# Layer 0's reciprocals spread over the partitions by two DMA transfers instead of a product

## The chip, the cores and the metric

The kernel runs on one core of one Trainium2 chip. The metric is the device time of one execution in microseconds (us), the median of several runs. The kernel before takes 924.37 us (three runs, 921.15 to 925.53). A profiled execution of the same kernel takes longer, 1061.9 us from the first to the last instruction; times read from the trace are on that longer scale.

## The reference

Two graph layers act on 2708 nodes with 256 features; `adj` is a weighted, sparse adjacency matrix of 2708 x 2708. Layer 0, which the change touches, computes per node j (cut to what matters):

```python
# per head h (3 of them): one logit per neighbour i, softmax over the row's edges
att = softmax(where(edge_adj > 0, e_plus, NEG_INF), axis=1)
support_h = (att * edge_adj) @ (h @ W_h)
edge_support = sum_h(support_h) / 3
node_support = adj_without_diagonal @ x
x = layernorm(x + diag * (gru(node_support, x) + gru(edge_support, x)))
```

The softmax is written as unnormalised weights, so each destination node needs a sum over its edges of weight times adjacency times features, per head, and the sum of the weights, the denominator. The support is the first divided by the second. Layer 1 is a second attention layer over the same graph with four heads, followed by another layer norm.

## The kernel before

Features lie on the partitions of the result (two halves of 128), destination nodes along the free axis. Destinations are cut into 43 **spans** of W0 = 64 (line 42; the last has 20), and eight spans make a **group** of 512; there are six groups, of which the last has 148 destinations in three spans. For each span the neighbours are collected into **tiles** of 128 rows: a few whole blocks (WHOLE0, line 43) and lists of gathered rows (TILES0, line 44). For each tile:

- `fetch_raw` (line 681) and `fetch_rows` (line 965) bring the adjacency values and the feature rows, by gathers that GpSimd issues, or by plain transfers on SyncE's queue for whole blocks;
- `prepared` (line 984) makes `four` on VectorE and ScalarE: the adjacency values, and the same times each of three head weights, side by side;
- `multiplied` (line 1016) multiplies the rows with `four` on TensorE and adds into the span's **sum bank** in PSUM (`sums[c]`, from a ring of two banks called acc), and adds the weights' counts into a **denominator bank** (`dens[c]`, from a ring of two called db).

When a span's last tile is in, `divided` (line 1045) works on it. VectorE adds up the denominators into `rden` (destinations on partitions, 64 x 3), replaces zeros, multiplies by the number of heads and takes reciprocals. The sums have features on partitions, so every partition needs every reciprocal: VectorE puts them on diagonals (`rden_own`, 64 x 192), TensorE multiplies these by a matrix of ones into a free part of the denominator bank, and ScalarE copies the result, 128 x 192, to `rb`. VectorE multiplies the three heads' sums, read from the sum bank, with `rb` and writes them to the group's `z` in SBUF. ScalarE has meanwhile copied the unweighted sums to `sa`. The sum bank can be reused when both are done.

After a group's last span `cells_and_norm` (line 1084) multiplies `z` with the head matrices (`supports`, line 1092), runs the two recurrent cells, normalises and projects for layer 1. Four groups find part of their gate products already computed and stored in DRAM (XH), and load them into working tiles on SyncE's queue (line 1127); such a load waits until its working tile is free. Group 4 and group 5 compute all of their gates there.

The order on each engine is not that of the source. Every call is noted, and a planner (`issue`, line 228) puts all instructions in order once, before the program is built: it keeps a model of each engine's time (for a transfer 2.2 us and its bytes at 250 GB/s, line 110), and on each engine takes, of what is ready in the model, what has the longest chain of work behind it. The result is a fixed order per engine. On the chip each engine, SyncE's queue too, runs its instructions in that order; an instruction that waits holds all that stand behind it on its engine. In the trace all these instructions carry the line of the recording helper (L217), so groups are told apart by tile names. `f_home` stands for several tiles that share a home in SBUF; z is one of them.

Of the kernel before, what the change touches and what calls it, by code (L numbers as in the profile page):

```python
# [10 lines left out]
F32 = mybir.dt.float32  # L11
# [9 lines left out]
P = 128  # L21
D = 256
KD = D // P
HEADS0 = 3
HEADS1 = 4
# [5 lines left out]
CH = 512  # L31
# [10 lines left out]
W0 = 64  # L42
# [264 lines left out]
def fast_path(ctx: ExitStack, tc: tile.TileContext, i: dict, out: bass.AP, bad: bass.AP):  # L307
# [11 lines left out]
    nc = plan = Plan(tc.nc)  # L319
# [8 lines left out]
    NG = len(groups)  # L328
# [3 lines left out]
    TW = D + 8  # L332
    C65 = C1 + 1
    H65 = HEADS1 * C65
    spans = [
        [(c * w, min(w, N - c * w)) for c in range((N + w - 1) // w)] for w in (W0, W1)
    ]
# [11 lines left out]
    dram = ctx.enter_context(tc.tile_pool(name="f_dram", bufs=1, space=DRAM))  # L349
# [16 lines left out]
    T0 = dram.tile([N, TW], F32, name="f_T0")  # L366
    T1 = dram.tile([N, TW], F32, name="f_T1")

    TS = dram.tile([NG, HEADS1, CH], F32, name="f_TS")

    KEPT = 4
    XH = dram.tile([KEPT * 2 * KD * 3 * P, CH], F32, name="f_XH")
    plan.pitch = {XH.tensor.name: CH, T0.tensor.name: TW, T1.tensor.name: TW, TS.tensor.name: HEADS1 * CH}


    home1 = const.tile([P, 12 * CH], F32, name="f_home1")
# [159 lines left out]
    small, lists = Rings(const, 2), Rings(const, 2)  # L536
# [156 lines left out]
    ap, tiles = Rings(const, 1, home2), Rings(const, 8, home1)  # L693
# [173 lines left out]
    for g, cs in enumerate(groups):  # L867
        w = width[g]
        pe, pf = accs[0], dbs[0]
        c0, nf = base[g] // W0, w // W0  # L870
        for b0 in range(0, NB, 2):
# [25 lines left out]
            for b in pair:  # L897
                if b in cs:
                    p, o = size[b], b * P - base[g]
# [16 lines left out]
            for b in pair:  # L916
                p = size[b]
# [3 lines left out]
            for b in pair:  # L921
                p = size[b]
# [120 lines left out]
    zs = {}  # L1043

    def divided(c):

        d0, w = spans[0][c]
        g = d0 // CH
        at = d0 - base[g]
        acc = sums[c]  # L1050
        rden = small.tile([W0, HEADS0], F32, name="rden")[:w]
        rb = small.tile([P, HEADS0 * W0], F32, name="rb")[:, : HEADS0 * w]
        own = small.tile([W0, HEADS0, W0], F32, name="rden_own")[:w, :, :w]

        if at == 0:
            zs[g] = (
                zp.tile([P, KD, CH], F32, name="sa", bufs=2), zp.tile([P, HEADS0, KD, CH], F32, name="z")
            )
        none = small.tile([W0, HEADS0], F32, name="none0")[:w]
        nc.vector.tensor_reduce(  # L1060
            rden, dens[c][:w, :H3].rearrange("p (s h) -> p h s", s=3), AX.X, ALU.add
        )

        nc.vector.tensor_scalar(none, rden, 0.0, None, op0=ALU.is_equal)
        nc.vector.scalar_tensor_tensor(rden, rden, float(HEADS0), none, op0=ALU.mult, op1=ALU.add)
        nc.vector.reciprocal(rden, rden)
        nc.scalar.copy(
            zs[g][0][:, :, at : at + w],
            acc.rearrange("p (o i) -> p o i", o=KD)[:, :, :w],
        )  # L1070
        nc.vector.tensor_mul(
            own, ident[:w, :w].rearrange("p (o i) -> p o i", o=1).to_broadcast([w, HEADS0, w]),
            rden.rearrange("p (h o) -> p h o", o=1).to_broadcast([w, HEADS0, w]),
        )
        pb = dens[c][:, P : P + HEADS0 * w]
        nc.tensor.matmul(pb, lhsT=ones_f[:w], rhs=own, start=True, stop=True, skip_group_check=True)
        nc.scalar.copy(rb, pb)
        nc.vector.tensor_mul(
            zs[g][1][:, :, :, at : at + w],
            acc.rearrange("p (o i) -> p o i", o=KD)[:, :, w : 4 * w].rearrange("p o (h i) -> p h o i", h=HEADS0),  # L1080
            rb.rearrange("p (h o i) -> p h o i", h=HEADS0, o=1).to_broadcast([P, HEADS0, KD, w]),
        )

# [145 lines left out]
    for n, (c, whole, m) in enumerate(work0):  # L1229
        if n == EARLY:  # L1230
            for k in slot1:
                fetch_mask(k)
        fetch_raw(n)
        fetch_rows(n)
        prepared(n)
        if multiplied(n):
            divided(c)
            d0, w = spans[0][c]
            if d0 + w in (base[g] + width[g] for g in range(NG)):
                cells_and_norm(d0 // CH)  # L1240
# [159 lines left out]
def tile_adj_resnorm(tc: tile.TileContext, i: dict, out: bass.AP):  # L1400
    nc = tc.nc
    with tc.tile_pool(name="guard", bufs=1) as gp:
        bad = gp.tile([P, 1], F32, name="bad")
        fast_path(tc, i, out, bad)
        with tc.tile_pool(name="guard_ps", bufs=1, space=PSUM) as ps:
            one = gp.tile([P, 1], F32, name="guard_ones")
            nc.vector.memset(one, 1.0)
            nc.vector.tensor_scalar(bad, bad, 0.0, None, op0=ALU.is_gt)
            n = ps.tile([1, 1], F32, name="n_bad")
            nc.tensor.matmul(n, lhsT=bad, rhs=one, start=True, stop=True)  # L1410
            flag = gp.tile([1, 1], I32, name="flag")
            nc.vector.tensor_copy(flag, n)
        taken = nc.values_load(flag[0:1, 0:1], min_val=0, max_val=P)
        with tc.If(taken > 0):
            general_path(tc, i, out)
# [436 lines left out]
```

## Time and profile before

| stretch of the trace, us | what runs | length, us | TensorE busy, us | GpSimd busy, us |
|---|---|---|---|---|
| 305 to 791 | layer 0's tiles, the groups' cells between them | 486 | 399.5 | 301.2 |
| 791 to 845 | group 4's cells | 54 | 54.0 | 0 |
| 845 to 856 | the last spans | 11 | 8.0 | 0 |
| 856 to 1062 | group 5's cells, layer 1 | 206 | 154.2 | 86.6 |

Before 305 us the adjacency matrix is read and the lists of neighbours are made. Over the whole span TensorE is busy 80%, VectorE 57%, ScalarE 53%, GpSimd 50%. A busy share is an average over stages: a wait in one stage is worth something only if TensorE, or what feeds it, has nothing else to do then. A line of a group gives busy time, mean length, and the idle time just before its instructions with what ended it. A line of waits gives who waited for whom, the total in us, how often, and the longest.

### The profile page before, as it was taken

To read this page: it belongs to the slowest core of one execution; us is meant where nothing else is said; L and a number is where in the kernel's file an instruction comes from. 1 tells how busy PE (TensorE), PEld (TensorE's weight loads), DVE (VectorE), ACT (ScalarE), POOL (GpSimd) and SP (SyncE) were. 2 spreads that over 40 slices of the span, in tenths; PEclk is the share of its full clock that TensorE was granted. 3 is DMA by queue.
4 is the path that set the end of the run, shared out by engine and by line. 5 is a ranking of instruction groups with operands and counts; after the bars stand their busy time and mean duration, and the time that the engine had idled before them with its cause. 6 is when DMAs were issued, how large, how long until landed. Compare 5 with 4: busy or idle time off the path is not lost.

```text
span 1061.9 us, 13987 instructions
## 1 busy us (share of the span) xinstructions
PE 847.5 (80%) x3911; PEld 518.9 (49%) x3911; DVE 605.2 (57%) x2035; ACT 557.7 (53%) x1568; POOL 530.5 (50%) x613
## 2 busy tenths in 40 slices
PE   5984888396888898859797698788989977977783
PEld 3431333133466653546345454553554557776672
DVE  5772588362155435847284326644841455988893
ACT  4783867374567653637345453553552232244486
POOL 2055557454466676866675565664430013466640
PEclk9996888698979789978897798899899988989996
DMA  8983878454433332433254223332220013545441
GB/s 306 300 266 98 270 247 236 117 151 105 160 102 85 85 90 79 139 95 104 73 168 143 76 60 97 111 97 77 76 78 0 1 41 99 158 127 152 145 120 52
DMA packets 85047, 132.41 MB, mean 125 GB/s; under 512 B 21520, under 2 KB 43880, under 8 KB 84320
## 3 DMA queue, kind: packets, MB, share of 16 engines
q1 hardware_dynamic: 56800, 71.68, 21.8%
q0 software_dynamic: 20320, 45.59, 16.5%
q10 hardware_dynamic: 7840, 14.16, 3.6%
q8 instruction: 33, 0.54, 0.2%
q14 instruction: 54, 0.44, 0.1%
HBM read 113.03 MB, written 21.12 MB: 126 GB/s over the span
## 4 chain that ended last, share of the span: by engine, by line
PE 35%; DVE 11%; issue 6%; ACT 5%; another core or an unknown queue 4%; DMA 2%; POOL 0%; ACTq 0%; DVEq 0%
PE side L217 17%; PE acc L217 12%; DVE f_home L217 7%; PE db L217 5%; ACT four L217 1%; ACT f_home L217 1%; DMA rows<-f_T,f_idx 1%; DVE f_xn L217 1%; DMA raw<-in_adj_dram,f_idx 1%; ACT y L217 1%; DVE four L217 1%; DVE rden L217 0%; PE pl L217 0%; ACT f_xn L217 0%
## 5 line engine op out<-in xcount | busy, mean ns | idle before, releaser
L217 POOL DMA_INDIRECT rows<-f_T,f_idx x254 | 255.6, 1006 | 276.9 <-PE side L217 91.9
L217 PE MATMUL acc<-four,rows 128*128 128x256 f32 (+1 forms) x712 | 214.1, 445 | 32.5 <-ACT four L217 17.6
L217 PEld LDWEIGHTS acc<-four,rows 128*128 128x128 f32 x712 | 147.9, 220 | 75.3 <-ACT four L217 23.7
L217 ACT ACTIVATE four<-four,rows 128x64 f32<-128x64 f32 (+1 forms) x534 | 145.3, 337 | 53.0 <-DVE four L217 17.0
L217 POOL DMA_INDIRECT raw<-in_adj_dram,f_idx x91 | 95.1, 1045 | 50.4 <-DVE f_m L217 26.2
L217 ACT ACTIVATE f_home<-f_home,f_minus_half 128x1024 bf16<-128x1024 f32 (+4 forms) x72 | 70.0, 976 | 50.3 <-remote 26.8
L217 POOL DMA_INDIRECT f_home<-in_adjT_dram,f_idx x67 | 64.5, 962 | 39.0 <-issue 17.1
L217 DVE TENSOR_REDUCE f_found<-f_home 128x16 f32<-128x1024 f32 (+5 forms) x84 | 72.4, 884 | 19.4 <-POOL f_home L217 9.8
L217 PE MATMUL db<-f_home,f_only 128*22 128x512 bf16 (+2 forms) x132 | 42.4, 404 | 46.9 <-ACT f_home L217 40.6
L217 PE MATMUL acc<-f_home,rows 128*65 128x128 f32 (+2 forms) x512 | 68.3, 286 | 11.1 <-DVE f_home L217 6.8
L217 POOL DMA_INDIRECT f_xn<-in_adjT_dram,f_idx x63 | 63.8, 1012 | 22.4 <-issue 17.4
L217 ACT ACTIVATE f_home<-f_home 128x1024 bf16<-128x1024 f32 (+4 forms) x72 | 62.9, 881 | 21.3 <-PE acc L217 8.1
L217 PE MATMUL side<-f_home,f_edge_wi 128*128 128x512 f32 (+1 forms) x144 | 62.7, 579 | 9.4 <-DVE f_home L217 5.3
L217 PEld LDWEIGHTS acc<-f_home,rows 128*65 128x65 f32 (+1 forms) x512 | 57.3, 144 | 18.1 <-DVE f_home L217 8.9
L217 PE MATMUL side<-f_home,f_node_wi 128*128 128x512 f32 (+1 forms) x144 | 62.3, 566 | 4.1 <-DVE f_home L217 4.1
L217 PE MATMUL side<-f_home,f_gat_w 128*128 128x512 f32 (+1 forms) x144 | 59.1, 569 | 3.8 <-DVE f_home L217 3.8
L217 DVE TENSOR_TENSOR f_home<-f_home,side 128x512 f32<-128x512 f32 (+1 forms) x56 | 36.6, 657 | 44.7 <-PE side L217 29.7
L217 DVE SCALAR_TENSOR_TENSOR f_home<-pl,rows,f_m 128x128 f32<-128x128 f32 x196 | 55.5, 341 | 9.9 <-DMA rows<-f_T,f_idx 5.4
L217 PE MATMUL db<-f_home,rows 128*65 128x128 f32 x376 | 51.5, 289 | 8.7 <-DVE f_home L217 7.3
L217 ACT ACTIVATE m<-four 128x64 bf16<-128x64 f32 (+1 forms) x181 | 40.9, 247 | 26.4 <-DVE four L217 21.2
L217 DVE SCALAR_TENSOR_TENSOR f_home<-ls,rows,f_m 128x128 f32<-128x128 f32 (+1 forms) x168 | 46.6, 339 | 4.8 <-PE side L217 2.8
L217 PEld LDWEIGHTS db<-f_home,rows 128*65 128x65 f32 x376 | 41.9, 143 | 14.9 <-DVE f_home L217 9.4
(221 smaller groups left out, 1458.9 us busy)
## 6 DMA issues: line engine op xcount, KB each, us to landing
f_home<-in_adjT_dram SPq DMA_DIRECT2D x50, 512.0 KB
f_XH<-kept ACTq DMA_DIRECT2D x48, 256.0 KB
f_home<-f_XH SPq DMA_DIRECT2D x48, 256.0 KB
f_home<-f_TS SPq DMA_DIRECT2D x5, 1024.0 KB
rows<-f_T SPq DMA_DIRECT2D x33, 132.0 KB
rows<-f_T,f_idx POOLq DMA_INDIRECT x254
f_T<-f_home SPq DMA_DIRECT2D x21, 132.0 KB
f_T<-in_x_dram SPq DMA_DIRECT2D x3, 896.0 KB
```

The costliest lines, as they stand in the source:

```text
L217: call = lambda: f(*args, **kwargs)
```

## The change

For all groups but the last, the reciprocals go to all partitions by way of DRAM: SyncE's queue writes `rden` (64 x 3) to a small DRAM tensor `f_TD`, and a second transfer, which waits for the first, reads these 192 numbers back onto each of the 128 partitions as `rb`. The diagonals, the product with ones and the copy of its result fall away. ScalarE copies the three heads' sums from the sum bank to `z` without waiting for the reciprocals, so that the bank depends on ScalarE alone, and VectorE multiplies `z` by `rb` in place. `rb` has a ring of three tiles, not two; the order of its 192 numbers is destination, then head. The last group's three spans are done as before.

```diff
+    TD = dram.tile([len(spans[0]) * W0, HEADS0], F32, name="f_TD")
...
-        rb = small.tile([P, HEADS0 * W0], F32, name="rb")[:, : HEADS0 * w]
-        own = small.tile([W0, HEADS0, W0], F32, name="rden_own")[:w, :, :w]
+        rb = small.tile([P, HEADS0 * W0], F32, name="rb", bufs=3)[:, : HEADS0 * w]
...
+        z = zs[g][1][:, :, :, at : at + w]
+        if g < NG - 1:
+
+            nc.sync.dma_start(TD[d0 : d0 + w, :], rden)
+            nc.scalar.copy(z, of_heads)
+            nc.sync.dma_start(
+                rb, bass.AP(tensor=TD.tensor, offset=TD.offset + d0 * HEADS0, ap=[[0, P], [1, w * HEADS0]])
+            )
+            nc.vector.tensor_mul(
+                z, z, rb.rearrange("p (o i h) -> p h o i", h=HEADS0, o=1).to_broadcast([P, HEADS0, KD, w])
+            )
+            return
+        own = small.tile([W0, HEADS0, W0], F32, name="rden_own", bufs=1)[:w, :, :w]
...
         nc.vector.tensor_mul(
-            zs[g][1][:, :, :, at : at + w],
-            acc.rearrange("p (o i) -> p o i", o=KD)[:, :, w : 4 * w].rearrange("p o (h i) -> p h o i", h=HEADS0),
+            z, of_heads,
             rb.rearrange("p (h o i) -> p h o i", h=HEADS0, o=1).to_broadcast([P, HEADS0, KD, w]),
         )
```

`of_heads` names the part of the sum bank that holds the three heads.

More of the change, by code (lines that the diff above doesn't have):

```diff
@@ L372, in fast_path @@
     XH = dram.tile([KEPT * 2 * KD * 3 * P, CH], F32, name="f_XH")
-    plan.pitch = {XH.tensor.name: CH, T0.tensor.name: TW, T1.tensor.name: TW, TS.tensor.name: HEADS1 * CH}
+    TD = dram.tile([len(spans[0]) * W0, HEADS0], F32, name="f_TD")
+    plan.pitch = {TD.tensor.name: HEADS0, XH.tensor.name: CH, T0.tensor.name: TW, T1.tensor.name: TW, TS.tensor.name: HEADS1 * CH}
     home1 = const.tile([P, 12 * CH], F32, name="f_home1")
@@ L1070, in divided @@
         )
+        of_heads = acc.rearrange("p (o i) -> p o i", o=KD)[:, :, w : 4 * w].rearrange(
+            "p o (h i) -> p h o i", h=HEADS0
+        )
[8 more added lines that the diff above has]
+                z, z, rb.rearrange("p (o i h) -> p h o i", h=HEADS0, o=1).to_broadcast([P, HEADS0, KD, w])
+            )
+            return
+        own = small.tile([W0, HEADS0, W0], F32, name="rden_own", bufs=1)[:w, :, :w]
         nc.vector.tensor_mul(
```

## The prediction

> **What bounds the kernel now.** I read the page's busy shares first, then busy time by stretches, then the engines' groups and waits of the stretch that the change touches, and last one span's chain in the timeline. The span sums of layer 0, and so the whole change, lie between 305 and 856 us of the profiled 1061.9 us; the timed runs last 924.37 us, so I scale what I find in the trace by 924.37 / 1061.9 = 0.870.
>
> Busy time by stretches (columns: start and end, length, then busy us and count for TensorE, its weight loads, VectorE, ScalarE, GpSimd; granted clock; DMA share; GB/s):
>
> ```profile
> 305.00:791.00 486.00, 399.53 (x1611) 249.94 (x1609) 263.72 (x889) 255.33 (x901) 301.21 (x296) 0.88 0.34 97
> 791.00:845.00 54.00, 54.00 (x128) 24.51 (x127) 13.41 (x22) 11.11 (x19) 0.00 (x0) 0.98 0.01 3
> 845.00:856.00 11.00, 7.96 (x41) 5.59 (x40) 9.99 (x37) 5.32 (x17) 0.00 (x0) 0.94 0.02 6
> ```
>
> TensorE is busy 82% of the first stretch and 100% of the second, where group 4's cells run alone. VectorE (54%) and ScalarE (53%) have room. GpSimd looks like 62%, but each of its gathers is followed by 0.30 us of issue, so 292 gathers of about 1.25 us make 365 us, 75%: the next limit, not far off. Groups of TensorE and ScalarE in 305 to 856 us (busy, mean ns, then the idle time before and what ended it):
>
> ```profile
> L217 PE MATMUL db<-rden_own,f_ones_f 64*128 64x192 f32 x84 | 26.1, 403 | 10.1 <-DVE rden L217 3.5 <-DVE rden_own L217 3.3 <-issue 3.2
> L217 ACT COPY rb<-db 128x192 f32<-128x192 f32 x42 | 12.9, 313 | 38.4 <-PE db L217 15.2 <-remote 10.8 <-issue 6.6
> L217 DVE TENSOR_TENSOR f_home<-acc,rb 128x384 f32<-128x384 f32 x42 | 22.8, 551 | 25.7 <-ACT rb L217 22.2 <-ACT f_home L217 1.1 <-issue 1.1
> L217 DVE TENSOR_TENSOR rden_own<-f_ident,rden 64x192 f32<-64x192 f32 x42 | 14.4, 348 | 0.4
> ```
>
> The first line is the product that spreads the reciprocals: 26.1 us of TensorE for 42 spans, 0.62 us each, and 10.1 us of idle time in front of it. Of the waits of TensorE in this stretch, two belong to the same chain:
>
> ```profile
> PE acc L217 <- DVE f_home L217: 10.1, 6, 6.9
> PE db L217 <- ACT rb L217: 1.0, 1, 1.0
> ```
>
> The tile view of rb puts the sum bank's share at 10.7 us for TensorE ("PE acc", 7 times). One span's chain shows why (start, length, engine, operation, and in brackets the idle time before):
>
> ```profile
> 503.34 0.29 PE L217 MATMUL db<-rows,m 128*64 128x9 bf16 x4
> 503.68 0.16 DVE L217 TENSOR_REDUCE rden<-db 64x3 f32<-64x9 f32 x1 [0.34 <-PE db L217]
> 504.71 0.35 DVE L217 TENSOR_TENSOR rden_own<-f_ident,rden 64x192 f32<-64x192 f32 x1
> 508.37 0.59 PE L217 MATMUL db<-rden_own,f_ones_f 64*128 64x192 f32 x2
> 514.29 0.32 ACT L217 COPY rb<-db 128x192 f32<-128x192 f32 x1 [3.10 <-PE acc L217]
> 514.64 0.56 DVE L217 TENSOR_TENSOR f_home<-acc,rb 128x384 f32<-128x384 f32 x1
> ```
>
> From the last count (503.63) to the end of the division (515.20) the span's sum bank, one of two, stays taken for 11.6 us.
>
> **What the Trainium skill says.** "DMA: Bandwidth & Descriptors", section on the anatomy of one DMA: some 2.0 us fixed per transfer, mostly the write's receipt, so a read that must wait for a write pays twice. Here the trace bears it out: after layer 0 the last rows of T1 have been issued by 868.18 and the gather that reads them begins at 870.50, 2.3 us; that gather lands in 2.73 us by the chain of work. "VectorE: DVE Perf Modes", section on the errata: ScalarE from PSUM to SBUF takes 172 cycles and one per element at 1.2 GHz. For 192 elements that is 303 ns; the trace has 313. So for 384, which no row here shows, 463 ns is my estimate. The same section gives (N + 151) / 0.96 ns for an fp32 tensor_tensor; 691 ns at 512, the trace 684 to 687, so 557 at 384 where both operands now lie in SBUF, against 551 from PSUM: no change.
>
> **The change part by part.** Five of the six groups, 40 of 43 spans, change.
> - TensorE loses 40 products, 40 x 0.62 = 25 us of busy time. TensorE is the limit for 82% of the stretch, so I count 25 x 0.82 = 20 us.
> - The waits attached to them end: 10.1 us in front of the product, 1.0 us of "PE db <- ACT rb", for the denominator bank whose free part ScalarE still had to copy. What TensorE runs next may be late itself, so I count half of the 11.1, 5 us, rounded down.
> - The sum bank is free after two ScalarE copies (0.26 and 0.46 us), not at the end of the chain: of the 10.7 us that TensorE waited for it I count 6, as half of what waits there also waits for new weighted masks (TensorE's longest wait in the stretch is 17.6 us for these). Copies and rb's ring of 3 are the only price.
> - VectorE loses 40 x 0.348 = 14 us (rden_own); ScalarE changes a 0.313 us copy for one of 0.463, 40 x 0.15 = 6 us more. Both engines are near 54%, and neither sets the end; zero.
> - SyncE issues 80 more transfers, each of some 0.3 us, and has room: by its own view of waits it stands 213.6 us waiting for VectorE to release buffers; zero for the engine. Bytes: 40 x (0.8 KB + 98 KB) = 4 MB against 97 GB/s in the stretch and over 250 GB/s early in the kernel; zero.
> - The new wait: the multiplication on VectorE needs the write's receipt and the read, 2.3 + 2.7 us and two issues of 0.3 us: 5.6 us after the reciprocal (bounds: 1.6 us twice the 0.8 us minimum round trip that the same page gives in its section on latency, and 9 us if each transfer takes double because of the 256 KB loads of kept gates queued ahead). Who waits behind it: the next weighted masks ("four") on VectorE, and so ScalarE, TensorE. In the changed program's order on VectorE there are 7 to 44 instructions between a reciprocal and its multiplication, 14 in the middle; 889 in 486 us are one per 0.55 us, so 14 are 7.7 us and cover it. Eight of the 40 have 10 or fewer, 5.5 us or less, and are short by 0 to 2 us; some others sit on SyncE behind gate loads that wait for buffers. I put 12 us of new VectorE waits, half of it reaching TensorE: 6 us lost.
> - Group ends: the products of the heads need the last span's z. In the changed order 2 to 5 tiles of the next group stand before them (1 to 2 before the change), each four products of 0.45 us, 1.8 us, so 3 more tiles are 5.4 us of useful work over the transfers; zero. The last group keeps its product, since nothing is left to hide a transfer there.
>
> Sum in the trace: 20 + 5 + 6 - 6 = 25 us. GpSimd takes some of it: its rows wait on the same buffers, and 486 - 25 = 461 us leaves it 79% occupied, so I take off a fifth: 20 us. Times 0.870: 17.4 us. Forecast 924.4 - 17.4 = 907 us.
>
> **Rivals.**
> - All of it comes through: 25 us of products, 10.1 and 10.7 us of waits, no new ones: 46 x 0.87 = 40, 884 us. For: TensorE 82% busy. Against: masks and gathers also end TensorE's waits.
> - The gathers become the limit: GpSimd's 75% occupancy leaves room, but its own waits ("rows" for row buffers, 34.8 us) do not all shrink; half of the forecast, 924.4 - 9 = 915 us.
> - The DMA wait takes the product's place: 40 multiplications each short by 1.5 us are 60 us on VectorE, of which 25 reach TensorE, and cancel the 25 gained: about 924 us. For: VectorE's wait for rb (22.2 us) exists already and only changes its source. Against: the distances above.
> - Slower: SyncE is in order and waits for buffers (the 213.6 us above); if reads of rb stand behind such loads at most spans, VectorE stalls by 3 us in 25 of 40 spans, 75 us, of which 40 reach TensorE: 25 + 5 + 6 - 40 = -4, and the reshuffled order of gathers adds as much again: some 8 x 0.87 = 7 us, 931 us.
>
> **How the numbers follow.** Forecast (895 to 914) 0.50; everything comes through 0.10; gathers 0.12; wash 0.12; slower 0.16. Faster by over 0.5% (below 919.8): 0.50 + 0.10 + 0.12 = 0.72; same 0.12; slower 0.16. The range takes in forecast, gathers and wash and reaches toward both ends: 888 to 930.
>
> **What would show it.** Right: products db<-rden_own only 6 records; "PE acc <- DVE f_home" near zero and replaced by short waits on ScalarE copies; TensorE's stretch before group 4's cells some 20 us shorter with 25 us less busy; VectorE waiting for rb in few, short pieces (12 us); the 54 us of group 4's cells unchanged. Wrong: VectorE idle before the multiplication by 40 us or more, SyncE holding rb's reads behind loads of kept gates, GpSimd's gathers back to back, or a first stage (to 300 us) that changes although nothing in it was edited, because the planner ranks all work anew.

## The result and the profile after

The kernel after takes 948.63 us (945.77 to 951.28) where the kernel before takes 924.7 us (921.15 to 925.53): a ratio of 1.0266 with a 95% interval of 1.0221 to 1.0311. It is slower by 2.7%; the prediction had 907 us and a range of 888 to 930, and gave "slower" 0.16.

In some sets of runs every kernel, the one before too, takes 1053 to 1111 us, with idle pieces of up to 20 us for which the trace shows no work to wait for, so each ratio below is to the kernel before in the same set and leaves out runs over 1.5% above the fastest of their kernel. The profile that the prediction read (1061.9 us) is such a long one; the profile of before used from here on spans 927.6 us. A long idle piece, in another profile of the kernel before, of 1092.6 us (start, length, instruction, and in brackets the idle time in front):

```profile
79.67 0.62 ACT L217 ACTIVATE f_home<-f_home 128x512 bf16<-128x512 f32 x1
97.46 1.15 ACT L217 ACTIVATE f_home<-f_home,f_minus_half 128x1024 bf16<-128x1024 f32 x1 [17.17 <-remote]
```

Where the time goes can be bounded by two events of the trace: the first span's denominators are added up, and group 4's cells begin (the first product with `f_gat_w`). Ahead of the first and behind the second little changes: the first lies at 258.8 us before and 257.3 after, and from the second to the same event of group 5 it is 74.6 and 74.9 us. Between the two lie 417.5 us before and 435.7 after (columns as in the prediction: busy us and count for TensorE, weight loads, VectorE, ScalarE, GpSimd; clock; DMA share; GB/s). The kernel before:

```profile
258.80:676.30 417.50, 374.32 (x1599) 235.05 (x1600) 263.82 (x887) 253.06 (x896) 299.14 (x293) 0.95 0.40 112
```

The kernel after:

```profile
257.30:693.00 435.70, 363.68 (x1551) 232.41 (x1549) 255.74 (x849) 259.13 (x909) 301.63 (x300) 0.92 0.57 117
```

TensorE is busy 10.6 us less and idle 28.8 us more (72.0 against 43.2). The DMA engines' share rises from 0.40 to 0.57 although they move hardly more bytes per second, 117 against 112 GB/s. The groups that the change touches, before:

```profile
L217 PE MATMUL db<-rden_own,f_ones_f 64*128 64x192 f32 x84 | 25.7, 397 | 7.3 <-DVE rden_own L217 7.2
L217 DVE TENSOR_TENSOR f_home<-acc,rb 128x384 f32<-128x384 f32 x42 | 22.8, 551 | 20.3 <-ACT rb L217 18.6 <-ACT f_home L217 1.4
```

and after:

```profile
L217 DVE TENSOR_TENSOR f_home<-f_home,rb 128x384 f32<-128x384 f32 x40 | 27.0, 678 | 54.8 <-DMA rb<-f_TD 38.4 <-ACT f_home L217 14.4 <-ACT four L217 1.9
L217 ACT COPY f_home<-acc 128x384 f32<-128x384 f32 x40 | 18.6, 466 | 4.8 <-PE acc L217 4.5
```

The 80 records of the product are gone, the ScalarE copy has come, and VectorE's idle time in front of the division has gone from 20.3 to 54.8 us, 38.4 of it for the read of `rb`. Waits by who waited for whom (us in total, times, longest), before:

```profile
ACT four L217 <- DMA rows<-f_T,f_idx: 26.0, 24, 5.5
PE acc L217 <- ACT four L217: 9.7, 13, 1.4
```

and after:

```profile
SPq L217 <- DMA f_TD<-rden: 83.9, 34, 4.8
ACT four L217 <- DMA rows<-f_T,f_idx: 40.8, 30, 3.7
DVE f_home L217 <- DMA rb<-f_TD: 38.4, 22, 4.5
PE acc L217 <- ACT four L217: 23.6, 22, 3.1
```

Besides VectorE's wait for `rb`, SyncE stands 84 us for the receipts of the writes, and a wait has grown in which none of the new transfers takes part: ScalarE for gathered rows, and TensorE for what ScalarE makes of them. The queues of the two kernels show why (packets, MB, share of the 16 DMA engines' span); before:

```profile
q1 hardware_dynamic: 56800, 71.68, 25.0%
q0 software_dynamic: 20320, 45.59, 19.3%
```

after:

```profile
q1 hardware_dynamic: 65760, 75.65, 28.8%
q0 software_dynamic: 20320, 45.59, 23.1%
```

q0 carries GpSimd's gathers. It has the same packets and bytes in both, but they take 23.1% of 945.0 us instead of 19.3% of 927.6: times 16 engines and over 20320 packets, 172 ns for one instead of 141. The new transfers are the 8960 packets more in q1, 224 for each of 40 spans. Two runs told of below make only one of the two transfers; they have 60000 and 62560 packets in q1, so 80 of the 224 belong to the write and 144 to the read.

One span's chain of work after, to be read against the one in the prediction (start, length, what), shows the new path from reciprocal to division:

```profile
498.91 0.18 DVE rden L217
499.09 0.02 issue
499.10 3.98 DMA f_TD<-rden
503.08 0.02 issue
503.10 5.21 DMA rb<-f_TD
```

The timeline has the division at the end of it, and the next span's reciprocal and transfers:

```profile
504.14 0.17 DVE L217 RECIPROCAL rden<-rden 64x3 f32<-64x3 f32 x1
504.34 0.45 SPq L217 DMA_DIRECT2D f_TD<-rden  x1
508.40 0.68 DVE L217 TENSOR_TENSOR f_home<-f_home,rb 128x384 f32<-128x384 f32 x1 [3.78 <-DMA rb<-f_TD]
508.53 0.32 SPq L217 DMA_DIRECT2D rb<-f_TD  x1
```

From the reciprocal's end, 499.09, to the division, 508.40, 9.3 us pass, and VectorE stood still for the last 3.78. SyncE meanwhile could pass nothing from 504.79, when the second write was issued, to 508.53, when its receipt let the second read go. Nine such trips on the chain between 480 and 700 us have a mean of 4.6 us for the write and 4.0 for the read.

### The profile page after: what moved, and what is told of

It is laid out like the page before. It is cut to its first block, busy times and chain, and to the rows that moved or that the text cites. A ratio compares the mean times of both kernels' runs of the same rounds, so it can differ in the third digit from the quotient of the medians.

```text
span 945.0 us, 13977 instructions
## 1 busy us (share of the span) xinstructions
PE 793.3 (84%) x3831; PEld 491.7 (52%) x3831; DVE 597.4 (63%) x1995; ACT 558.4 (59%) x1567; POOL 531.4 (56%) x613
## 3 DMA queue, kind: packets, MB, share of 16 engines
q1 hardware_dynamic: 65760, 75.65, 28.8%
q0 software_dynamic: 20320, 45.59, 23.1%
## 4 chain that ended last, share of the span: by engine, by line
PE 42%; DMA 21%; DVE 16%; ACT 8%; issue 7%; POOL 5%; SPq 0%; ACTq 0%; DVEq 0%; POOLq 0%
PE side L217 19%; PE acc L217 13%; DVE f_home L217 10%; PE db L217 9%; DMA f_TD<-rden 6%; DMA rb<-f_TD 5%; DMA rows<-f_T,f_idx 5%; POOL f_m L217 3%; DMA raw<-in_adj_dram,f_idx 3%; ACT four L217 2%; ACT f_home L217 2%; PE pl L217 1%; ACT y L217 1%; DMA f_home<-in_L_gnn_gat_a_dram 1%; DVE f_xn L217 1%
## 5 line engine op out<-in xcount | busy, mean ns | idle before, releaser
L217 PE MATMUL acc<-four,rows 128*128 128x256 f32 (+1 forms) x712 | 202.5, 427 | 28.0 <-ACT four L217 23.6
L217 PEld LDWEIGHTS acc<-four,rows 128*128 128x128 f32 x712 | 142.2, 211 | 77.9 <-ACT four L217 32.5
L217 POOL DMA_INDIRECT f_home<-in_adjT_dram,f_idx x67 | 65.7, 980 | 20.3 <-issue 15.7
L217 DVE TENSOR_TENSOR f_home<-f_home,rb 128x384 f32<-128x384 f32 x40 | 27.0, 678 | 54.8 <-DMA rb<-f_TD 38.4
L217 PE MATMUL side<-f_home,f_node_wi 128*128 128x512 f32 (+1 forms) x144 | 59.8, 547 | 1.3 <-DVE f_home L217 1.3
L217 PE MATMUL side<-f_home,f_edge_wi 128*128 128x512 f32 (+1 forms) x144 | 57.9, 545 | 0.0
L217 PE MATMUL db<-f_home,rows 128*65 128x128 f32 x376 | 49.3, 283 | 5.8 <-DVE f_home L217 5.8
L217 DVE TENSOR_TENSOR f_home<-f_home,side 128x512 f32<-128x512 f32 (+1 forms) x56 | 36.6, 657 | 17.9 <-PE side L217 17.5
L217 PE MATMUL acc<-f_home,f_home 128*9 128x512 bf16 (+2 forms) x132 | 40.0, 385 | 8.9 <-ACT f_home L217 8.9
```

What stands on the lines that cost most here:

```text
L217: call = lambda: f(*args, **kwargs)
```

## The experiments

In kernels said to have "the order kept", the planner is told of the same operations as in the kernel it is made from, so every engine has the same order; only what is issued in their place differs. They leave something out or read fixed numbers, which is said of each. Medians of all runs, and ratios to the kernel before of the same set:

| run | before, us | this, us | ratio (95%) |
|---|---|---|---|
| after, again | 922.31 | 951.69 | 1.0287 (1.0232 to 1.0343) |
| early copy only | 922.31 | 922.18 | 0.9983 (0.9958 to 1.0007) |
| before, without the product | 922.31 | 915.16 | 0.9925 (0.988 to 0.997) |
| transfers made, none waits | 925.74 | 941.16 | 1.0178 (1.0114 to 1.0243) |
| transfers left out | 925.74 | 914.85 | 0.9898 (0.9873 to 0.9923) |
| read need not wait for the write | 925.74 | 941.91 | 1.0204 (1.0137 to 1.027) |
| transfers priced in the planner | 925.74 | 937.74 | 1.0113 (1.0074 to 1.0152) |

A ratio is not quite the quotient of the two medians beside it: for the read that need not wait, four runs between 932 and 948 us, that quotient is 1.0175. The runs of the longer sets have no line here; their ratios stand with them below. My theory at this point was that the waits for the round trip, VectorE's above all, cost the time; the rivals were the changed order and the transfers' presence as such.

**Removing each wait, order kept.** Three kernels. The first reads `rb` from other data, so that the read doesn't wait for the write; the second makes both transfers but divides by fixed numbers, so that VectorE waits for neither; the third leaves the transfers out as well. (All three divide by other numbers than the reference's.)

```diff
+            other = bass.AP(tensor=x.tensor, offset=x.offset + c * D, ap=[[0, P], [1, w * HEADS0]])
-            nc.sync.dma_start(
-                rb, bass.AP(tensor=TD.tensor, offset=TD.offset + d0 * HEADS0, ap=[[0, P], [1, w * HEADS0]])
+            plan.note(
+                "sync", "dma_start", lambda to, _: tc.nc.sync.dma_start(to, other),
+                (rb, bass.AP(tensor=TD.tensor, offset=TD.offset + d0 * HEADS0, ap=[[0, P], [1, w * HEADS0]])), {},
             )
```

```diff
-            nc.vector.tensor_mul(
-                z, z, rb.rearrange("p (o i h) -> p h o i", h=HEADS0, o=1).to_broadcast([P, HEADS0, KD, w])
-            )
+            of_rb = lambda v: v.rearrange("p (o i h) -> p h o i", h=HEADS0, o=1).to_broadcast([P, HEADS0, KD, w])
+            fixed = of_rb(gat_w[:, 0, 0, : HEADS0 * w])
+            plan.note(
+                "vector", "tensor_mul", lambda to, v, _: tc.nc.vector.tensor_mul(to, v, fixed), (z, z, of_rb(rb)), {}
+            )
```

```diff
-            nc.sync.dma_start(TD[d0 : d0 + w, :], rden)
+            plan.note("sync", "dma_start", lambda to, v: None, (TD[d0 : d0 + w, :], rden), {})
...
-            nc.sync.dma_start(
+            plan.note(
+                "sync", "dma_start", lambda to, v: None,
...
```

They ran first, beside a profile of the kernel before, in a set in which the kernel before takes 1086 us.

> The kernel before, unchanged, profiled a second time. Its first profile spans 1061.9 us where its timed runs last 924; that of the changed kernel spans 945.0 where its runs last 949. If the first profile was stretched, this one should span some 920 to 930 us, with about 465 us or less from the first sums to group 4's cells, and gathers spaced more tightly. If it spans 1060 again, profiling costs this kernel 140 us that it doesn't cost the changed one.

> The changed kernel with the order of every engine kept, in which the transfer to rb reads 192 numbers of the input x and so doesn't wait for the write of the reciprocals (the result is then divided by other numbers). Both transfers are still made. Latency theory (waits for the round trip hold VectorE and the ends of the groups): SyncE's 84 us of waits for the write go, rb comes some 4 us earlier, so about half of the loss returns and more: 920 to 935 us. Traffic theory (the 80 small transfers slow down the gathers): no change, 945 to 950. Order theory (the planner's new order is the loss): 940 to 950.

> The changed kernel with the order of every engine kept and both transfers made, but VectorE multiplies by fixed numbers (a row of the head weights) and so waits for no transfer (the result is then not divided by the sums of weights). Latency theory: the whole loss and the hoped for gain appear, 900 to 915 us. Traffic theory: 940 to 950, since the transfers are all there. Order theory: 940 to 950.

> As the run before, and the two transfers of each span are left out too; the order of every engine is kept. What it gains over the run before is the traffic and SyncE's waits. Latency theory: within 5 us of the run before, 900 to 912. Traffic theory: 900 to 915, some 30 us below the run before. Order theory: 935 to 950, since nothing but the order is left of the change.

They gave 1.0187 (1.0082 to 1.0293), 1.0092 (1.0062 to 1.0122) and 0.9914 (0.9867 to 0.996). The same three kernels, in a set in which the kernel before takes 925.74 us, with a fourth that is told of further below:

> The changed kernel, order of every engine kept, both transfers made, VectorE multiplying by fixed numbers so that it waits for neither (the result is not divided by the sums of weights); the same kernel as the second of the first set, now beside runs of some 925 us. Latency theory (38 us of VectorE's waits for rb, and TensorE's behind them): ratio 0.98 to 0.995, the whole 2.7% gone. Traffic theory (the DMA share rose from 0.39 to 0.57 in the stretch, ScalarE's waits for gathered rows from 26.0 to 40.8 us): 1.02 to 1.03. Order theory: 1.02 to 1.03.

> As the run before, with both transfers of each span left out as well, order kept. Latency theory: 0.98 to 0.99, within 0.005 of the run before. Traffic theory: 0.98 to 0.995, at least 0.02 below the run before. Order theory: 1.01 to 1.03, as there is nothing left but the order and the copies. What this run and the one before differ by is the price of the traffic.

> The changed kernel, order kept, both transfers made, rb read from the input x and so not after the write (the result is divided by other numbers). The wait for the write's receipt, some 4.6 us of the 8.6 us round trip, goes. Latency theory: half of the loss or more returns, ratio 1.00 to 1.015. Traffic and order theory: 1.02 to 1.03.

The third, with the transfers left out, is 1.0% faster than before in the order of the kernel after: the order isn't what costs. Making the transfers, with no engine but SyncE waiting for them, takes it from 0.9898 to 1.0178, 941.16 - 914.85 = 26.3 us. The wait of VectorE, which the theory had made the main cost, is what remains from 1.0178 to the 1.0266 and 1.0287 of the whole change: 0.9 to 1.1%, 8 to 10 us. That is a rough figure, since it compares sets whose ratios are each uncertain by some 0.5 points. So the theory falls; the presence of the transfers costs most. In the kernel without transfers the stretch up to group 4's cells reads

```profile
258.80:660.60 401.80, 349.04 (x1557) 221.95 (x1555) 257.54 (x855) 258.92 (x912) 307.39 (x299) 0.97 0.43 117
```

33.9 us less than after: TensorE is idle 52.8 us, not 72.0, and its 1557 products are 14.6 us shorter than the 1551 after, at a granted clock of 0.97 against 0.92. The waits tell the same; where transfers are made and none waits for them:

```profile
SPq L217 <- DMA f_TD<-rden: 87.9, 34, 5.0
ACT four L217 <- DMA rows<-f_T,f_idx: 50.3, 32, 9.0
```

where they are left out:

```profile
ACT four L217 <- DMA rows<-f_T,f_idx: 22.5, 26, 2.8
```

where the read doesn't wait for the write:

```profile
ACT four L217 <- DMA rows<-f_T,f_idx: 49.0, 29, 3.7
DVE f_home L217 <- DMA rb<-in_x_dram: 10.3, 12, 2.3
```

The last kernel has no wait of SyncE for receipts at all, 28 us less of VectorE's wait, and is still 1.0204; the wait for gathered rows stays at twice its length. Its SyncE still stands for the reciprocals that it writes, 67.1 us in 19 waits, against 35.0 us in 14 in the kernel after.

**The change's parts without the transfers.** Beside the kernels before and after, one that only takes the early copy over (ScalarE copies the heads' sums to `z`, VectorE multiplies there, the product stays; the planner gives it an order of its own), and one that takes the product, its diagonals and its copy out of the kernel before, order kept, for the five groups, and divides by fixed numbers.

```diff
         nc.scalar.copy(rb, pb)
+        if g < NG - 1:
+            nc.scalar.copy(z, of_heads)
         nc.vector.tensor_mul(
-            zs[g][1][:, :, :, at : at + w],
...
+            z, z if g < NG - 1 else of_heads,
```

```diff
...
-        nc.tensor.matmul(pb, lhsT=ones_f[:w], rhs=own, start=True, stop=True, skip_group_check=True)
-        nc.scalar.copy(rb, pb)
+        plan.note(
+            "tensor", "matmul", lambda *of, **how: tc.nc.tensor.matmul(*of, **how) if kept else None,
+            (pb,), dict(lhsT=ones_f[:w], rhs=own, start=True, stop=True, skip_group_check=True),
+        )
+        plan.note("scalar", "copy", lambda *of: tc.nc.scalar.copy(*of) if kept else None, (rb, pb), {})
...
```

> The kernel before, profiled once more. On another chip its time was 1086 us, 17% above the 924.7 us of the comparison with the changed kernel, and its profile showed engines idle for up to 20 us with nothing in the trace to wait for. If this run's time is near 925, its profile is the one to lay beside that of the changed kernel (945.0 us): layer 0's sums should then take about 440 to 450 us, and the gathers should stand at most 1.3 us apart where they are the limit.

> The changed kernel again, beside the others of this set. A ratio of 1.02 to 1.03 if the chip behaves as in the first comparison; where runs last 1080 us and more, long idle pieces hide waits that end at the same time, and the ratio should lie nearer 1, 1.00 to 1.02.

> One part of the change alone: ScalarE copies the heads' sums out of their bank at once and VectorE divides them in place, while the reciprocals are spread by the product as before. Latency theory: the part without transfers can only help, by the bank's waits (10.7 us counted before), less some 6 us of ScalarE: ratio 0.985 to 1.00. Order theory: anything from 0.98 to 1.03, since the planner ranks all work anew. Traffic theory: as the latency theory.

> The kernel before with the order of every engine kept, and for five of six groups without the diagonals, the product and the copy of its result; VectorE multiplies by fixed numbers instead (the result is not divided by the sums of weights). This is the most that taking the product out can give, with nothing in its place. The prediction counted 31 us in the trace before new waits, some 27 us timed: ratio 0.965 to 0.975. If the product hides beside GpSimd's gathers, 0.985 to 1.00, and the gain that the prediction set against the new waits was never there.

The copy alone changes nothing that can be measured (0.9983). Taking the product out with nothing in its place gains 0.75%, 7 us (the interval allows 3 to 11), of 25.7 us of TensorE's busy time and 7.3 us of waits in front of it. In this order, that is the most the change had to gain from this part; the kernel without transfers (0.9898) has the early copy and the new order too, and gains 11 us by the medians; the intervals overlap.

**The transfers' times told to the planner.** The planner counts 2.2 us and the bytes for a transfer. Given 2.4 us more for the write and 1.8 for the read, it puts more instructions between a reciprocal and its division: 24 in the middle of VectorE's order, not 14. The longer times also count in its ranking of chains. This kernel computes all.

```diff
+    def more(op):
...
+        return 2.4 if op.out.startswith("f_TD") else 1.8 if op.out.startswith("rb") else 0.0
...
-                end = moved
+                end = moved + self.more(op)
```

> The changed kernel complete, with the planner told that the write takes 2.4 us and the read 1.8 us longer than any transfer does in its model (4.6 and 4.0 us from issue to landing, as the trace of the changed kernel has them). In the new order 24 instructions stand between a reciprocal and its multiplication on VectorE in the middle of the spans, 14 before. Latency theory: most of the loss was that the order allows the transfers too little time, so 0.99 to 1.01. Traffic theory: 1.015 to 1.03.

It is the best of the complete kernels with the transfers, 1.0113, and still slower than before. The tile view of `rb` in its profile has what is left of VectorE's wait in front of the division (us, times):

```profile
  DMA rb<-f_TD: 0.2, 1
```

and the waits have ScalarE's for the rows:

```profile
ACT four L217 <- DMA rows<-f_T,f_idx: 45.8, 22, 4.0
```

So the order can hide the round trip from VectorE entirely. The gathers' wait remains, and so do 69.3 us of SyncE's waits for receipts. The gain over the kernel after, 1.5 points, is larger than the 0.9 to 1.1 put down to VectorE's wait above; every engine has a new order here, and no run separates that from the shorter wait.

**Which transfer, and what of it.** Over all runs, a gather's packet (share of q0 times span times 16, over 20320) takes:

| what the queue carries for 40 spans | ns per gather packet |
|---|---|
| none of the transfers | 141, 138 and 141 (before; the last two in longer sets), 143 (early copy), 142 (no product), 145 and 143 (transfers left out) |
| write of 64 rows of 12 bytes and read | 172 and 169 (after), 179 and 171 (none waits), 171 and 161 (read at once), 180 (planner) |
| the same write of constants, and a read that waits for nothing | 166 |
| write of 64 rows of 12 bytes alone | 182, 166 |
| read alone, one row onto 128 partitions | 147 |
| read alone, 128 different rows of 768 bytes | 145 |
| write of one row of 768 bytes, and read | 138 |

The five last lines are kernels made for this, order kept, dividing by fixed numbers; as the kernel that leaves both out, with one or both transfers issued again, from or to other places. Writes alone and reads alone take over one of the diffs above each; for the reads of 128 rows the source's step from partition to partition is `D`, not 0. In the first of the five, traffic alone, the write takes constants, and nothing on SyncE waits for a reciprocal or a receipt:

```diff
-            nc.sync.dma_start(TD[d0 : d0 + w, :], rden)
+            plan.note(
+                "sync", "dma_start", lambda to, _: tc.nc.sync.dma_start(to, ident[:w, :HEADS0]),
+                (TD[d0 : d0 + w, :], rden), {},
+            )
```

In the last, the write is one long row of constants, the read waits for it, and VectorE waits for neither:

```diff
-            nc.sync.dma_start(TD[d0 : d0 + w, :], rden)
+            line = bass.AP(tensor=TD.tensor, offset=TD.offset + d0 * HEADS0, ap=[[w * HEADS0, 1], [1, w * HEADS0]])
+            plan.note(
+                "sync", "dma_start", lambda to, _: tc.nc.sync.dma_start(line, gat_w[0:1, 0, 0, : w * HEADS0]),
+                (TD[d0 : d0 + w, :], rden), {},
+            )
```

> The changed kernel, order kept, both transfers of each span made with the same bytes and shapes, but the write sends constants and the read takes numbers of the input x, and VectorE multiplies by fixed numbers: neither SyncE nor VectorE waits for them (the result is not divided by the sums of weights). Traffic theory: as with nobody waiting for data, 1.012 to 1.02. Queue theory (SyncE's waits for reciprocals and for the write hold the loads behind them): 0.99 to 1.00, as without transfers.

> Order kept, the write of the reciprocals made, the read left out, VectorE multiplying by fixed numbers (the result is not divided by the sums of weights). The write is 64 rows of 12 bytes. Traffic theory, if the small rows are what loads the DMA engines: 1.01 to 1.02. If the read does: 0.99 to 0.995. Queue theory: 0.995 to 1.005, as SyncE still waits for the reciprocals but not for the write.

> Order kept, the write left out, the read made from one row of the input x onto all partitions with nobody waiting, VectorE multiplying by fixed numbers (the result is not divided by the sums of weights). 128 packets of 768 bytes. Traffic theory, if the read loads the DMA engines: 1.01 to 1.018. If the write does: 0.99 to 0.995. Queue theory: 0.99, nothing is waited for.

> As the run before, but each partition reads another row of x, 768 bytes of it; bytes and packets are the same (the result is not divided by the sums of weights). If it is the one row read 128 times at once that holds the DMA engines: back to 0.99 to 0.995. If it is packets and bytes: as the run before.

> The changed kernel, order kept, both transfers made and the read waiting for the write, but the write sends 768 bytes of constants from one partition as one row in place of 64 rows of 12 bytes, and VectorE multiplies by fixed numbers (the result is not divided by the sums of weights). If the small rows hold up the gathers: gather packets at 143 to 150 ns, the ratio at 0.99 to 1.00 although SyncE still waits for every write. If any write does, or the reads: 165 ns and more, 1.01 to 1.02 where runs last 925 us. If SyncE's waits for the write were the cost: 145 ns, but 1.01 or more.

> The write alone again, order kept, 64 rows of 12 bytes, no read, VectorE multiplying by fixed numbers (the result is not divided by the sums of weights). Small rows theory: gather packets at 175 to 185 ns as before, and where runs last 925 us a ratio of 1.005 to 1.02. If the read or SyncE's waits for the write were needed for the loss: 0.99 to 1.00 at the same packet time.

The packets settle which transfer lengthens them: the write in 64 rows of 12 bytes lengthens the gathers' packets from a mean of 142 ns to between 161 and 182, by 13 to 28%, whoever waits for it; the reads (145 and 147), and the same 768 bytes written as one row (138), hardly do. "DMA: Bandwidth & Descriptors" in the Trainium skill states under Specifications that below 512 bytes the engine reads, modifies and writes. No run here shows that step itself, and the write as one row makes 2 packets where the small rows make 80, so the size of the rows and their number are not told apart. What the table adds is that another queue's packets pay.

The times don't settle how much of the 26 us that is. These ran where the kernel before takes 1094 and 1072 us: traffic alone 0.9977 (0.9945 to 1.0009), writes alone 1.0028 (0.9995 to 1.0061) and, the same kernel in the second set, 1.0097 (1.0062 to 1.0133), reads alone 0.9951 (0.9905 to 0.9997), reads of rows 0.9958 (0.9927 to 0.9988), long row 1.0146 (1.01 to 1.0192). By the medians of all runs the long row would be 1.0051, and in the first set the transfers left out 1.0052 and not 0.9914: these ratios cannot rank the kernels. As they stand, traffic alone has the slow packets and no loss; the long row has fast packets, SyncE still waiting for receipts (14.7 us), and a loss. Read so, the cost would be SyncE's queue standing still; but at 925 us the kernel whose SyncE waits for no receipt lost 1.0204 - 0.9898 = 3.1%, about 1.1 points of which the 10.3 us of VectorE's wait could explain at most. That does not exclude the held queue, because SyncE stands for the reciprocals there. One and the same kernel differs by 0.007 between two such sets, as much as what is to be told apart.

The traces of the 925 us set say where the loss arrives. Up to group 4's cells, all engines together wait 24.6 us for gathered rows where the transfers are left out, and 51.9 where they are made and none waits for them; for everything that SyncE's own queue carries they wait 2.4 and 10.2 us. On the chain of work of that stretch, a gather takes a mean of 3.4 us from issue to landing in the first (14 gathers) and 4.9 in the second (16). So most of the loss reaches the engines through the gathers, and little through loads held up on SyncE. That it is the longer packets that make the gathers late fits this, but is not shown: in the longer sets traffic alone has the long packets, and ScalarE waits 17.4 us for rows there, against 17.9 with the transfers left out. None of the five kernels ran at 925 us, so the split between slower gathers and SyncE's held queue stays open.

## Why the prediction was wrong

The prediction set a gain of 31 us in the trace against a loss of 6. Of the gain 7 to 11 us exist; of the loss, the transfers' presence alone makes 26 us, and VectorE's wait for them 8 to 10. The steps that failed are the two zeros for the transfers, as bytes and as work on SyncE's queue, and the size of the product's term. How the 26 us divide between the two zeros stays open.

- **"20 us" for the product: mis-sized, by about a factor of three.** TensorE's busy time did fall as said, but "the limit for 82% of the stretch" took a busy share for a share of the path. With nothing in the product's place the timed gain is 7 us, where 20 and the 5 for its waits came to 25 x 0.87 = 22. Between before and the kernel without transfers TensorE's busy time falls by 25.3 us up to group 4's cells and its idle time rises by 9.6: part of the gain becomes waiting.
- **"6" for the sum bank: nothing.** The mechanism is there ("PE acc <- DVE f_home", 4.3 us up to group 4's cells, is gone in the kernel with the early copy alone, with 0.3 us for ScalarE's copy in its place), but that kernel is 0.9983. TensorE waits for the weighted masks instead, 19.4 us and not 9.1, as the step half allowed.
- **"Bytes: 4 MB against 97 GB/s ... zero": the first step that failed.** The write is 0.8 KB, but 64 rows of 12 bytes in 80 packets, and the transfers' presence costs 26 us with no engine but SyncE waiting for them. Bandwidth was not the resource: 117 GB/s after, 112 before, while the DMA engines' share rose from 0.40 to 0.57, the gathers' packets grew from 142 ns to between 161 and 182, and the waits for gathered rows doubled.
- **"SyncE has room ... zero for the engine": failed as an argument, of open size.** 213.6 us of standing for buffers isn't room in a queue that runs in order: it now stands 84 us for receipts as well. What engines wait for on that queue's other transfers is small, 10.2 us against 2.4.
- **"5.6 us after the reciprocal": too short.** 4.6 + 4.0 us, near the upper bound of 9. The 2.3 us came from the stretch after layer 0, where no gathers ran. Fourteen instructions, 7.7 us, then don't cover it; VectorE waited 38.4 us, not 12, and by the difference above 8 to 10 us, not 6, reach the time.
- **"Group ends: zero": failed.** Before group 4's cells (start, length, instruction) the kernel before needs 2.9 us from the last reciprocal to the first product:

```profile
673.45 0.16 DVE L217 RECIPROCAL rden<-rden 64x3 f32<-64x3 f32 x1
674.75 1.02 DVE L217 TENSOR_TENSOR f_home<-acc,rb 128x384 f32<-128x384 f32 x2 [0.55 <-ACT rb L217]
676.33 1.45 PE L217 MATMUL side<-f_home,f_gat_w 128*128 128x512 f32 x3
```

  The chain of work after has both transfers there (the last reciprocal began at 683.14):

```profile
683.57 4.69 DMA f_TD<-rden
...
688.27 3.95 DMA rb<-f_TD
...
692.25 0.67 DVE f_home L217
...
692.99 7.20 PE side L217 x11
```

  That is 9.9 us, and in the 11 us from 682.5 TensorE is idle for 3.6, where the kernel before is idle 0.4 us in the 13 from 664.5.
- **"557 ... no change" for VectorE's division: 678 ns.** In place with `rb` in its old order (the early copy alone) it is 553, so the prediction's price held for the move from PSUM to SBUF. The 125 ns come with the new order of `rb`, read at every third number: with fixed numbers at the same step and no transfers, it is still 675. 40 x 0.125 = 5 us on an engine with room. ScalarE's copy, 463 ns by the prediction's estimate from the Trainium skill, "VectorE: DVE Perf Modes" (errata), is 466.
- **Times 0.870: a wrong scale.** It spread the 138 us between the profile and the timed runs evenly over the trace. The stretch of 486 us is 417.5 in a profile that spans as long as the timed runs; there TensorE is busy 90%, not 82, and the 365 us that the prediction counted for GpSimd's gathers would be 87%, not 75: the next limit stood nearer than it looked.
- The slower rival named SyncE's order and got 931 us from waits alone; it had the right sign, but it too had no term for the transfers' traffic. Group 4's cells (54.0 us of TensorE in both) and the first stage stayed as predicted, and the product is left with its six records.

In sum, as ratios to before: everything but the transfers -1.0%, their presence +2.8, the division's wait for them +0.9 to 1.1; together +2.7 to 2.9. The last of the three is the remainder, not measured alone.

## What to carry to other kernels

Price a transfer by its rows and packets and by what else runs on the DMA engines and stands in its queue, not by its bytes alone, and take the length of a trip from a stretch with the same traffic. Before replacing an operation, ask what the kernel gains with nothing in its place: an engine's busy share is an upper bound, and here the prize was 7 us, or 11 with the early copy and the new order. See that a profile's span agrees with the timed runs before scaling from it.

## What the runs showed that I had not expected

- Forty small writes to DRAM in 64 rows of 12 bytes make the 20320 packets of another queue 13 to 28% longer (161 to 182 ns against a mean of 142); as one row each they do not (138 ns).
- An fp32 operand read at a stride of 12 bytes costs VectorE 678 ns for 128 x 384 results where the same multiplication in order takes 553.
- TensorE's granted clock was 0.913 to 0.921 in all eight runs of the kernel after and 0.928 to 0.948 in those of the kernel before near 925 us; its products of 128 x 256 (TensorE's largest group) took a mean of 431 ns after, 423 before and 401 with the transfers left out, in 258 to 658 us. The Trainium skill, "TensorE: Matmul & The Clock Gate", Part 1, says that the clock follows how busy the engine has been. The kernel after fits that up to group 4's cells (72.0 us idle at 0.92, before 43.2 at 0.95), but the kernel with the transfers left out does not (52.8 us idle at 0.97), so what lowers the clock here stays open.
